# Moving the second matrix's threshold of one group from the mixing stage into the inverse rounds

## The chip, the cores and the metric

One core of a Trainium2 chip runs the program. Its five engines work through instruction queues of their own: PE (matrix products), DVE, ACT and POOL (elementwise work) and SP, which here only issues DMAs. An instruction starts when it is at the head of its engine's queue and everything it waits for is done. The metric is the device time of one execution in microseconds.

## What is computed

Four layers act in turn on a tensor of 4 images x 64 channels x 256 x 256 in float32. Layers 0, 2 and 3 are long convolutions along rows and columns with generated filters, plus a bias times the input; the kernel computes them as products with Toeplitz matrices. Layer 1 is the one that the change touches:

```python
f1 = haar2d(x)
acc = jnp.zeros_like(f1[:, :conv_w.shape[1]])
for i in range(v.shape[0]):
    f3 = f1 * v[i]
    f4 = jnp.einsum('bchw,oc->bohw', f3, conv_w[i])
    f5 = jnp.sign(f4) * jax.nn.relu(jnp.abs(f4) - tau[i])
    acc = acc + f5
y = haar2d(acc, inverse=True)
return y + x
```

`v[i]` and `tau[i]` depend on the position in the image only, not on the channel, so the product with `v[i]` may come after the channel mixing as well as before it. `sign` times `relu(abs - tau)` is the shrinking (soft threshold) that the title speaks of. There are two matrices, and the last addition of x is done in the Haar domain too.

## The kernel before

The four images are two groups of two. A **round** holds two channels of the two images of a group, 128 partitions x 8 blocks x 256 columns; there are 32 rounds per group, 64 in all. Three pieces of program are woven together:

- `phase_a` (lines 405 to 505): for each round the first convolution and the forward Haar transform. It writes Haar coefficients to a tensor `coef` in device memory, one per group.
- `phase_b` (507 to 678): the channel mixing. It needs all channels of a position, so it goes through `coef` in 64 **steps** per group, each of 128 partitions x 2 images x 512 positions. A step is two **units**, one for each of the two matrices. A unit is a product with the matrix on PE (`mix`), then on a tile of 128x1024: the product with v (`multiply`, DVE), `sign` and `magnitude` (ACT), the subtraction of tau (`less`, DVE), the threshold (`threshold`, DVE, a scalar_tensor_tensor), and the addition (`add`, POOL; for the first unit the addition of x in two halves, for the second one addition of 128x1024). `store` writes the step's sum to a tensor `mixed`. Each unit is three entries in a list; `exchange` is a copy on ACT, once a step. `load_f` and `load_v` bring the next steps' coefficients, v and tau, two DMAs for the coefficients and one each for v and tau.
- `phase_c` (680 to 808): for each round the inverse Haar transform and the two last convolutions. It loads g from `mixed`, undoes the free-axis part of the Haar transform on POOL (`inverse_free`, line 340: sixteen additions and subtractions, a pair per level, each level twice as long as the one before, the last two of 128x1024), with scalings of g's parts on ACT (line 353) ahead of each level, does the partition part on PE (`product`, c0ps), and then per layer a row stage (`rows`, c1r and c2r) and a column stage (`columns`, c1c and c2c) on PE. Row results are copied out of PSUM by ACT (line 733), column results by DVE with the bias term (line 752), Haar results by ACT and, for the second group, half by DVE (line 721).

The order of every engine's queue is the order in which this program writes its instructions. A round of `phase_c` is eighteen pieces: four of c1r, one Haar product, four of c2r (of the round before), the other Haar product, four of c1c, four of c2c. At the start of a piece `flush` writes the PSUM copies that the piece before left waiting; then come loads and stores, the PE work, and one step of the inverse Haar of the round two further on (`step(t + 2, 1)`, two pieces per level). `sums(t + 2)`, in the round's first piece, sets that inverse Haar up.

PSUM banks for the convolutions come in pairs from `rings`: during the mixing of the second group two pairs, in the last stage four (`rings[:] = [acps, acps, wide, wide]`). A product waits until the pair it is to write has been copied out.

`beside` weaves two lists: it spreads the second list's entries evenly over the first's. The mixing of the first group runs beside the forward rounds of the second. The mixing of the second group runs beside the first `cut_c` pieces of the inverse rounds:

```python
cut_a, cut_c = (ROUNDS + 2) * A_PIECES + BLOCKS + 1, (ROUNDS - 2) * C_PIECES
...
beside(main, phase_b(1), len(c_first) + len(a_end) + 2 * BLOCKS, 0)
during.close()
wide = pool("wide2", 4, space=PSUM)
rings[:] = [acps, acps, wide, wide]
beside(c[cut_c:], [], 0, 0)
```

So 30 of the inverse rounds run beside mixing; the others, with what is left of the last, run alone. That is the last stage.

## Time and profile before

| what | value |
|---|---|
| median of 3 runs | 2615.12 us (2614.1 to 2617.48) |
| the profiled execution | 2622.7 us, of which the span from the first to the last instruction 2620.6 us |
| busy share of the span: PE, DVE, ACT, POOL | 90%, 64%, 51%, 74% |
| granted PE clock, mean | 0.965 |
| moved by DMA | 631.58 MB, 241 GB/s in the mean |
| issues of v and tau | 128 each, 512 KB each, 5.9 and 6.6 us to landing |
| issues of mixed (stores), g (loads) | 256 each, 256 KB each, 5.9 and 5.5 us to landing |

The span has four stretches: forward rounds of the first group (to some 450 us), forward rounds of the second beside mixing of the first (to some 1130 us), inverse rounds beside mixing of the second group (to some 1950 us), and inverse rounds alone (to the end). In lines of the profile, L579 stands for line 579 of the kernel; `out<-in` names tiles; `x` ahead of a number is a count.

### The profile page before, as it was taken

Reading aid. Unit: us, or ns where it says so; the run is one execution under the profiler, and the core shown is the slowest. Engines: PE = TensorE matmul, PEld = TensorE weight load, DVE = VectorE, ACT = ScalarE, POOL = GpSimd, SP = SyncE. Lnnn points to the kernel's source line nnn. Section 1 sums busy time; section 2 is a strip of 40 time slices with the busy share of each in tenths; the row PEclk is TensorE's granted clock in tenths of the full one; section 3 lists DMA queues with packets and bytes.
Section 4 is the critical chain, followed back from the end, with each engine's and each line's share of the span. In section 5 each row is a group of like instructions: output and inputs, shape, how many; then the busy total and the mean of one; then the engine's idle time right before and its main releaser. Section 6 shows DMA issues by size and latency. Waiting matters only on the chain.

```text
span 2620.6 us, 120068 instructions
## 1 busy us (share of the span) xinstructions
PE 2357.1 (90%) x53276; PEld 1908.0 (73%) x53276; DVE 1686.6 (64%) x1972; ACT 1325.3 (51%) x2169; POOL 1951.1 (74%) x2422
## 2 busy tenths in 40 slices
PE   6989999678878778768999999999999999999999
PEld 4777777445544445546877777787789999999999
DVE  2464445799999999736877878878763333333333
ACT  1111112566666656426777776778763443434432
POOL 2877887888989989858888878888876565565661
PEclk9999999899899888979999999999999999999999
DMA  5756887698999889556888878888865544445442
GB/s 147 252 193 221 254 261 275 232 332 326 336 332 335 319 316 331 186 190 216 286 310 288 295 273 288 274 285 286 284 231 181 171 143 153 159 141 166 148 137 86
DMA packets 241180, 631.58 MB, mean 241 GB/s; under 512 B 42758, under 2 KB 125351, under 8 KB 224536
## 3 DMA queue, kind: packets, MB, share of 16 engines
q1 hardware_dynamic: 240664, 623.92, 69.4%
q8 instruction: 419, 6.86, 1.1%
q14 instruction: 97, 0.79, 0.1%
HBM read 412.59 MB, written 211.16 MB: 238 GB/s over the span
## 4 chain that ended last, share of the span: by engine, by line
PE 42%; DVE 12%; DMA 10%; POOL 9%; ACT 6%; issue 5%; SPq 2%; DVEq 0%; ACTq 0%; POOLq 0%
PE c1c L285 9%; PE c2r L285 9%; PE c2c L285 8%; PE c1r L285 8%; PE c0ps L297 3%; DVE a L605 3%; PE f L579 3%; DVE x L594 3%; POOL f L335 2%; POOL fw L333 2%; DVE m L608 2%; DMA ft<-coef 2%; ACT a L602 2%; DMA mixed<-gt 2%; DVE x L449 2%
## 5 line engine op out<-in xcount | busy, mean ns | idle before, releaser
L370 POOL TENSOR_TENSOR i<-i,g 128x16 f32<-128x16 f32 x744 | 395.1, 550 | 378.9 <-ACT g L353 359.9
L579 PE MATMUL f<-ft,mix 64*64 64x512 f32 x2048 | 326.4, 642 | 106.7 <-DVE x L594 84.5
L285 PEld LDWEIGHTS a1ps<-tx,x 64*64 64x64 f32 x8192 | 303.4, 140 | 132.9 <-DVE f L462 47.8
L602 ACT ACTIVATE a<-x 128x1024 f32<-128x1024 f32 x256 | 264.5, 1033 | 205.6 <-DVE m L608 205.6
L285 PE MATMUL a1ps<-tx,x 64*64 64x192 f32 (+3 forms) x8192 | 341.5, 309 | 29.3 <-DVE f L462 15.3
L605 DVE TENSOR_TENSOR a<-a,tau 128x1024 f32<-128x1024 f32 x256 | 314.3, 1228 | 79.9 <-ACT a L602 77.5
L285 PEld LDWEIGHTS c2r<-tx,cy 64*64 64x64 f32 x8192 | 319.1, 135 | 62.2 <-ACT ch L733 28.8
L598 ACT ACTIVATE m<-x 128x1024 f32<-128x1024 f32 x256 | 271.9, 1062 | 173.3 <-DVE x L594 112.4
L594 DVE TENSOR_TENSOR x<-f,v 128x1024 f32<-128x1024 f32 x256 | 311.7, 1218 | 61.1 <-PE f L579 56.4
L285 PEld LDWEIGHTS c1c<-ty,ch 64*64 64x64 f32 x8192 | 311.3, 133 | 53.4 <-ACT ch L733 29.8
L285 PE MATMUL c2r<-tx,cy 64*64 64x64 f32 (+3 forms) x8192 | 330.9, 301 | 13.6 <-ACT ch L733 10.9
L285 PE MATMUL c1r<-tx,z 64*64 64x128 f32 (+3 forms) x8192 | 326.7, 299 | 13.1 <-DMA tx<-filt 6.7
L285 PEld LDWEIGHTS c1r<-tx,z 64*64 64x64 f32 x8192 | 303.0, 134 | 46.4 <-issue 26.4
L285 PEld LDWEIGHTS a2ps<-ty,ay 64*64 64x64 f32 x8192 | 281.4, 135 | 74.1 <-issue 27.2
L285 PE MATMUL a2ps<-ty,ay 64*64 64x256 f32 (+3 forms) x8192 | 319.1, 301 | 12.5 <-ACT ay L429 9.1
L285 PE MATMUL c1c<-ty,ch 64*64 64x192 f32 (+3 forms) x8192 | 321.1, 298 | 7.0 <-ACT ch L733 6.2
L608 DVE SCALAR_TENSOR_TENSOR m<-a,m 128x1024 f32<-128x1024 f32 x256 | 313.0, 1223 | 19.5
L429 ACT COPY ay<-a1ps 128x512 f32<-128x512 f32 x256 | 137.0, 587 | 370.7 <-PE a1ps L285 370.3
L285 PE MATMUL c2c<-ty,ch 64*64 64x192 f32 (+3 forms) x8192 | 316.4, 297 | 3.6 <-issue 3.6
L285 PEld LDWEIGHTS c2c<-ty,ch 64*64 64x64 f32 x8192 | 303.2, 133 | 22.4 <-issue 10.9
L449 DVE SCALAR_TENSOR_TENSOR x<-x,bias_sb,a2ps 128x512 f32<-128x512 f32 x256 | 179.4, 743 | 214.1 <-POOL f L335 132.1
L620 POOL TENSOR_TENSOR gt<-gt,m 128x1024 f32<-128x1024 f32 x128 | 303.2, 2369 | 11.7 <-DVE m L608 10.2
(69 smaller groups left out, 3193.9 us busy)
## 6 DMA issues: line engine op xcount, KB each, us to landing
coef<-f SPq DMA_DIRECT2D x256, 256.0 KB, 4.4
ft<-coef SPq DMA_DIRECT2D x256, 256.0 KB, 6.2
v<-in_v SPq DMA_DIRECT2D x128, 512.0 KB, 5.9
tau<-in_tau SPq DMA_DIRECT2D x128, 512.0 KB, 6.6
mixed<-gt SPq DMA_DIRECT2D x256, 256.0 KB, 5.9
g<-mixed SPq DMA_DIRECT2D x256, 256.0 KB, 5.5
x<-in_x SPq DMA_DIRECT2D x63, 1024.0 KB, 8.5
out<-o SPq DMA_DIRECT2D x63, 1024.0 KB, 5.1
```

Source lines behind the costliest of these rows:

```text
L285: nc.tensor.matmul(ps[r][half(c), j % 2, k * ROW :], data[half(r), c, k, bass.ts(j, ROW)], t(r, c)[:, : N - k * ROW], start=k == 0, stop=k ...
L297: nc.tensor.matmul(ps[r][half(c)].rearrange("p h k -> p (h k)"), matrix[half(r)], pairs(r, c).rearrange("p h k -> p (h k)"), start=True, s ...
L370: engine.tensor_tensor(to, s, d, op)
L429: later(lambda y=y, ps=ps: nc.scalar.copy(y, ps))
L449: nc.vector.scalar_tensor_tensor(to, old, bias_sb[:, c : c + 1], ps, ALU.mult, ALU.add)
L579: nc.tensor.matmul(un[u]["f4"][half(q), b, :], mixers[0][half(r), bass.ts(i, C)], st[s]["f"][half(r), b], start=True, stop=True, tile_posi ...
L594: nc.vector.tensor_tensor(un[u]["x"], un[u]["f4"], both(u, "v"), ALU.mult)
L598: nc.scalar.activation(un[u]["m"], un[u]["x"], AF.Sign)
L602: nc.scalar.activation(un[u]["a"], un[u]["x"], AF.Abs)
L605: nc.vector.tensor_tensor(un[u]["a"], un[u]["a"], both(u, "tau"), ALU.subtract)
L608: nc.vector.scalar_tensor_tensor(un[u]["m"], un[u]["a"], 0.0, un[u]["m"], ALU.max, ALU.mult)
L620: nc.gpsimd.tensor_tensor(st[s]["g"], st[s]["g"], m, ALU.add)
```

## The change

For the second group, and for steps from `FULL` = 2 on, the second unit of a step no longer shrinks. Its product with the matrix is copied from PSUM to a tile `raw` by DVE and stored to a new tensor `unshrunk`; v, sign, magnitude, tau, threshold and addition are left out there. For the second matrix v and tau are no longer loaded in those steps. For the first two steps the second unit is done as before, and zeros are stored in `unshrunk`. (These two steps are joined with one another in `join` and `part`.)

In the last stage the rounds of the second group load their rows of `unshrunk` (`load_raw`), and `shrink` does the product with v, sign, magnitude, subtraction and threshold in two halves of 128x1024, in the pieces of the round three ahead (`AHEAD`), with tiles of v and tau in the rounds' own layout that are loaded once (`v_rows`, `tau_rows`). `x`, the intermediate, lies in PSUM, one buffer of two banks. `sums` adds the two halves to g on POOL before the inverse Haar.

Mixing of the second group now runs beside 29 inverse rounds, not 30. The last stage has three pairs of PSUM banks, not four. The load of g for round 32 is no longer set apart.

```diff
-    cut_a, cut_c = (ROUNDS + 2) * A_PIECES + BLOCKS + 1, (ROUNDS - 2) * C_PIECES
+    cut_a, cut_c = (ROUNDS + 2) * A_PIECES + BLOCKS + 1, (ROUNDS - AHEAD) * C_PIECES
...
+        def raw(u):
+            return grp == GROUPS - 1 and u % 2 == 1 and FULL <= u // 2 < STEPS
...
+                d[name] = []
+                for i in range(2 if s < FULL else 1):
+                    t = bp.tile([P, W], F32, tag=f"{name}{i}", name=f"{name}{i}_{grp}_{s}", bufs=3 - 2 * i)
+                    d[name].append(t)
+                    nc.sync.dma_start(t, bass.AP(src.tensor, at + i * W, [[n, P], [1, W]]))
...
         def multiply(u):
+            if raw(u):
+                t = st[u // 2]["raw"] = bp.tile([P, NB, W], F32, tag="raw", name=f"raw_{grp}_{u}", bufs=2)
+                nc.vector.tensor_copy(t, un[u]["f4"])
+                return
...
         def store(s):
             for to, g in step_of(mixed[grp], s, st[s]["g"]):
                 nc.sync.dma_start(to, g)
+            if grp == GROUPS - 1:
+                if s < FULL:
+                    t = st[s]["raw"] = bp.tile([P, NB, W], F32, tag="raw", name=f"none_{grp}_{s}", bufs=2)
+                    nc.gpsimd.memset(t, 0.0)
+                for to, g in step_of(unshrunk, s, st[s]["raw"]):
+                    nc.sync.dma_start(to, g)
...
+        def load_raw(t):
+            if alone <= t < total:
+                r = st[t]["raw"] = late["sb"].tile([P, 2 * M, N], F32, tag="raw", name=f"raw_{t}", bufs=2)
+                for rows, to in all_rows(unshrunk, t % ROUNDS, r):
+                    nc.sync.dma_start(to, rows)
+
+        def shrink(t, j):
+
+            if j < 0 or not alone <= t < total:
+                return
+            h, j = divmod(j, SHRINK)
+            s = st[t]
+            at = [s[k].rearrange("p (s b h) k -> p s b (h k)", s=2, b=NB)[:, h] for k in ("raw", "shrunk") if k in s]
+            if j == 0:
+                if h == 0:
+                    s["shrunk"] = late["sb"].tile([P, 2 * M, N], F32, tag="shrunk", name=f"shrunk_{t}", bufs=2)
+                s["x"] = late["ps"].tile([P, NB, W], F32, tag="x", name=f"x_{t}_{h}")
+                nc.vector.tensor_tensor(s["x"], at[0], late["v"][:, h].unsqueeze(1).to_broadcast([P, NB, W]), ALU.mult)
+            elif j == 1:
+                nc.scalar.activation(at[1], s["x"], AF.Sign)
+            elif j == 2:
+                nc.scalar.activation(s["x"], s["x"], AF.Abs)
+            elif j == 4:
+                by = late["tau"][:, h].unsqueeze(1).to_broadcast([P, NB, W])
+                nc.vector.tensor_tensor(s["x"], s["x"], by, ALU.subtract)
+            elif j == 5:
+                nc.vector.scalar_tensor_tensor(at[1], s["x"], 0.0, at[1], ALU.max, ALU.mult)
...
         def sums(t):
             if t < total:
                 s = st[t]
+                if t >= alone:
+                    for h in range(2):
+                        to, of = (s[k].rearrange("p (s n) k -> p s (n k)", s=2)[:, h] for k in ("g", "shrunk"))
+                        nc.gpsimd.tensor_tensor(to, to, of, ALU.add)
                 s["ci"] = big("t1", f"ci_{t}", 2)
...
-                if t == alone - 2:
-                    load(alone)
                 sums(t + 2)
...
-            if j == 2 * BLOCKS and t + 3 != alone:
+            if t >= alone - AHEAD:
+                if j == 0 and t == alone - AHEAD:
+                    load_raw(alone)
+                if j == BLOCKS:
+                    load_raw(t + AHEAD + 1)
+                shrink(t + AHEAD, order.index(j) - 2)
+            if j == 2 * BLOCKS:
...
-    wide = pool("wide2", 4, space=PSUM)
-    rings[:] = [acps, acps, wide, wide]
+    rings[:] = [acps, acps, pool("wide2", 2, space=PSUM)]
+    late["sb"] = pool("late", 1)
+    late["ps"] = pool("late_ps", 1, space=PSUM)
+    for name, src in (("v", v_rows), ("tau", tau_rows)):
+        t = late[name] = late["sb"].tile([P, 2, W], F32, tag=name, name=f"{name}_rows")
+        for r in range(2):
+            nc.sync.dma_start(t[half(r)].rearrange("p s w -> p (s w)"), src)
     beside(c[cut_c:], [], 0, 0)
```

`AHEAD` is 3, `SHRINK` 8, `FULL` 2. In the later steps the guards `if raw(u): return` stand in `sign`, `magnitude`, `less`, `threshold` and `add` as well.

## The prediction

> **What bounds the kernel now.** I first read the page's forty slices to find the stages, then busy time by stretch. The first line below is the stretch in which the second group's mixing runs beside the first group's inverse rounds; the second is the last stage, inverse rounds alone. Columns: stretch, its length, then busy us and instruction count (x) of PE, PEld, DVE, ACT, POOL, then granted clock, DMA share, GB/s.
>
> ```profile
> 1200.00:1950.00 750.00, 706.77 (x15688) 579.78 (x15684) 592.12 (x599) 563.34 (x908) 628.78 (x643) 0.99 0.80 279
> 1957.00:2572.00 615.00, 612.96 (x16807) 587.97 (x16803) 222.87 (x318) 246.75 (x547) 364.25 (x512) 1.00 0.49 153
> ```
>
> An inverse round issues 528 matmul records (four times 128 in the convolutions, 16 in the Haar product). The last stage holds 16807/528 = 31.8 rounds, **19.3 us each**, with PE idle for 2 us of 615: PE sets the end there. In the mixing stretch the side list has 404 pieces for 532 main pieces, which is 13.67 per round or 2.28 steps (a step is six pieces, two units); with 16 records a step a round has 564, so 15688/564 = 27.8 rounds, **27.0 us each**. PE, DVE, POOL and ACT are all 75 to 94% busy there: no single engine, but queues in fixed order that wait on each other.
>
> Next the order of time in one round of the last stage, since an engine's queue order decides what new work costs there.
>
> ```profile
> 2214.11 4.02 POOL L370 TENSOR_TENSOR i<-i,g 128x256 f32<-128x256 f32 x4 [1.37 <-ACT g L353]
> 2214.32 1.71 ACT L353 ACTIVATE g<-g 128x512 f32<-128x512 f32 x3
> ...
> 2218.20 4.72 POOL L370 TENSOR_TENSOR ci<-i,g 128x1024 f32<-128x1024 f32 x2
> ...
> 2221.97 4.48 PE L285 MATMUL c1r<-tx,z 64*64 64x256 f32 x124
> 2222.17 1.41 DVE L752 SCALAR_TENSOR_TENSOR o<-cy,bias_sb,c2c 128x512 f32<-128x512 f32 x2 [0.78 <-PE c2c L285]
> ...
> 2224.41 1.07 ACT L733 COPY ch<-c1r 128x512 f32<-128x512 f32 x2 [8.38 <-PE c1r L285]
> ...
> 2227.10 4.58 PE L285 MATMUL c2r<-tx,cy 64*64 64x256 f32 x125
> ```
>
> PE starts a round at 2221.97 and its second row stage 5.1 us later. POOL finishes the previous inverse Haar at 2222.92, 0.95 us *into* the round. ACT's third scaling in the row at 2214.32 is already the first of the next round's: ACT runs ahead, then idles 8.38 us. Two more views, groups by shape and SP's rows in order of time:
>
> ```profile
> L620 POOL TENSOR_TENSOR gt<-gt,m 128x1024 f32<-128x1024 f32 x128 | 303.2, 2369 | 11.7 <-DVE m L608 10.2 <-POOL gt L624 0.3
> L594 DVE TENSOR_TENSOR x<-f,v 128x1024 f32<-128x1024 f32 x256 | 311.7, 1218 | 61.1 <-PE f L579 56.4 <-DMA tx<-filt 4.6
> L598 ACT ACTIVATE m<-x 128x1024 f32<-128x1024 f32 x256 | 271.9, 1062 | 173.3 <-DVE x L594 112.4 <-POOL gt L620 28.7 <-POOL gt L624 12.5
> L602 ACT ACTIVATE a<-x 128x1024 f32<-128x1024 f32 x256 | 264.5, 1033 | 205.6 <-DVE m L608 205.6
> ```
>
> ```profile
> 1499.33 1.70 SPq L692 DMA_DIRECT2D g<-mixed  x2
> 1501.23 3.11 SPq L149 DMA_DIRECT2D tx<-filt  x4
> 1504.46 1.59 SPq L149 DMA_DIRECT2D ty<-filt  x2
> 1506.10 2.50 SPq L149 DMA_DIRECT2D tx<-filt  x4
> 1508.70 2.06 SPq L149 DMA_DIRECT2D ty<-filt  x2
> 1510.85 1.18 SPq L629 DMA_DIRECT2D mixed<-gt  x2
> ```
>
> SP issues 16 DMAs in 12.7 us, back to back, 0.79 each.
>
> **What leaves the mixing stretch.** Of a step's second unit go three DVE instructions (product 1.22, subtraction 1.23, threshold 1.22), sign and magnitude on ACT (1.06 + 1.03) and one POOL addition (2.37). In their place comes one DVE copy from PSUM, which this trace does not show at 128x1024: between the product of that shape, 1.22, and twice the 128x512 copy, 1.38; I take 1.22, the nearer in shape. Net per step: DVE 2.45, ACT 2.1, POOL 2.4. The two zero tiles for steps 0 and 1 are one memset each on POOL, about 1.15 us by elements from the 80x320 memset of 0.36 us, hidden in POOL's 16% of idle; without that cover 2 us.
>
> What it adds there: SP. A step issues six DMAs now (ft, mixed two each, v and tau one each) and eight after, two stores more; v and tau are halved, so the bytes stay. And the stretch is one round shorter (29 rounds beside mixing, not 30): 404/514 x 18/6 = 2.36 steps per round. With 17 DMAs of the inverse round itself (12 filters, 4 g, 1 out) SP issues 17 + 2.36 x 8 = **35.9 per round**, against 17 + 2.28 x 6 = 30.7 now. At the back-to-back price above that is 28.4 us; at the best row (4 in 2.50 us, with the gap to the next 0.65 each) 23.3. PE's floor is the 19.3 plus 4.72 units at 0.76 to 1.09 us (a Haar product's stretch alone; the eight mixing records end to end): 22.9 to 24.4. Now SP's 30.7 fit in 27.0, so not all are 0.79. I take 0.71 for a DMA, midway, and **25.5 us per round**, SP the last to finish; bounds 23.3 and 27.0 (no gain). Behind SP's queue stand ft, v, tau, g and the filters, which all wait when it is full.
>
> Stretch: 28 rounds x 27.0 = 756 become 27 x 25.5 = 688.5, and one round, the first alone, at about 24: 19.3 plus 5 (bounds 0 and 12), because the first product in it waits for the last store to land (5.9 us in the table of DMA issues), then for a load (5.5), with the DVE evacuations queued behind it. Together **-43.5**; with both bounds -108 and +4.
>
> **What the last stage receives.** In each of 32 rounds: on DVE two products, subtractions and thresholds (7.3 us), on ACT two signs and magnitudes (4.2), on POOL two additions, 4.72 us as the row at 2218.20; on SP four loads, 21 DMAs x 0.8 = 17 us of a round, issued a round ahead. By busy sums all fits: POOL 364/31.8 = 11.5 + 4.7 = 16.2, ACT 7.8 + 4.2, DVE 7.0 + 7.3. PSUM rings go from four bank pairs to three.
>
> By order it does not fit. The two additions stand at the head of a round on POOL, behind the previous Haar's tail; the first ACT scaling of that round (L353, on the same g) must wait for both; behind it on ACT stand the evacuations of c1r, which free the banks of the second row stage, and the later scalings, which POOL's tail waits for. So there is a **loop**, POOL to ACT to POOL, and its length is a floor for the round:
>
> - additions: 4.7;
> - ACT from the first scaling to the sixth: 6 scalings (0.23 to 0.65, 2.2 in all), 8 evacuations of 0.59, 2 z copies of 0.60, 2 signs of 1.06, 1 magnitude of 1.03 = 11.3, less 19 overlaps of 0.11 (copies at 2224.41 are 1.07 for two): 9.2. The second sign waits for the second product, which on DVE follows subtraction, threshold and a z copy, all after the magnitude: +0.6;
> - POOL's last four operations: 2 x 1.28 + 4.72 = 7.2.
>
> Sum **21.8**, against 19.3. ACT cannot run ahead any more; PE waits some 2.5 us at its second row stage.
>
> One thing more. The moved product reads raw and v, both from SBUF; before, every large DVE operation beside POOL had one operand in PSUM. The trace has DVE operations with two SBUF operands, with POOL still (first row) and with POOL busy:
>
> ```profile
> 129.17 2.14 DVE L205 SCALAR_TENSOR_TENSOR u<-k,u 128x512 f32<-128x512 f32 x3
> 158.61 2.07 POOL L335 TENSOR_TENSOR f<-x 128x1024 f32<-128x1024 f32 x1
> 158.97 5.16 DVE L205 SCALAR_TENSOR_TENSOR u<-k,u 128x512 f32<-128x512 f32 x3
> ```
>
> Three take 2.14 us in the one case and 5.16 in the other: they take turns with POOL. In the new round the first product falls among POOL's tail or additions, which run without a gap, so POOL loses its 1.2 us; the second falls where POOL has gaps. Loop **23.0** (bounds 21.2, with neither wait, and 23.6, with both products paid).
>
> The Trainium skill, page "SBUF — State Buffer", section "SBUF: two separate sides", calls this an exclusive lock: a DVE operation with two SBUF inputs and a GpSimd one that reads SBUF exclude each other for a whole instruction. By that rule both products would cost POOL 1.2 us whenever POOL is busy, 24.2 a round, some 38 us more than my sum. The page "DMA: Bandwidth & Descriptors", section "Issuing engines are not separate DMA queues", holds the time to initiate a DMA to be usually small; by it SP would drop out and the mixing round stand at PE's 23 to 24 us, 50 us below my sum; the SP rows above speak against it.
>
> Last stage: 32 x (23.0 - 19.3) = **+118** (bounds +61 and +138).
>
> **Sum.** -43.5 + 118 = +75. The profiled execution ran 2622.7 us with a span of 2620.6, and the runs' median is 2615.1, so on the median: 2615 + 75 = **2690 us**.
>
> **Rivals.**
> *A, the other side: the loop does not close.* If POOL's additions fit into its idle (41% of the last stage, 7.9 us a round, more than 4.7) and the last stage keeps 19.3, the mixing stretch at 24 us a round decides: 27 x 24 + 24 - 756 = -84, **2531**. For it: busy sums, and DVE, ACT and POOL all get lighter beside mixing. Against: POOL's idle lies after ACT's scalings ("<-ACT g L353"), not before them. It decides once 32 x (loop - 19.3) is below 732 - 27r for a mixing round r: at r = 25.5 a loop below 20.7, at 23.3 below 22.5.
> *B, SP fills up.* Mixing stays at 27.0 a round: -3 + 118, **2730**. For: 0.79 each, 28.4 us. Against: a lighter POOL and DVE end the waits inside SP's queue sooner.
> *C, no turns with POOL.* DVE's product finds a gap: loop 21.8, +80 - 43.5, **2652**. For: ACT waits long enough for a late product; against: the rows above.
>
> **Chances.** Forecast (2670 to 2715) 0.42, B 0.20, C 0.20, A 0.15, and 0.03 for gain and loss to cancel. The range reaches from the near edge of cancelling to past B: 2612 to 2745, which leaves out A and a little above. A measurement of this kernel tells about 0.2% (5 us) from no change: faster 0.15, same 0.03, slower 0.82.
>
> **What would show it.** In the changed profile the last stage's c1r stages should stand 22 to 23.5 us apart; the second row stage should wait for ACT; ACT's first scaling should wait for a POOL addition; POOL should be over 70% busy with its tail running straight into the additions; the products should last over 1.22 us wherever POOL runs. In the mixing stretch SP should issue almost without gaps and a round take 24.5 to 26.5. I am wrong if c1r stays 19 to 20 us apart, or if the mixing round falls below 24.

## The result, and the profile after

| | before | after |
|---|---|---|
| median of 4 runs each | 2616.3 us (2614.1 to 2618.02) | **2900.16 us** (2899.37 to 2903.64) |
| ratio after/before, 95% interval | | **1.109** (1.107 to 1.111): slower by 284 us |
| span of the profiled execution | 2620.6 us | 2897.6 us |
| granted PE clock, mean | 0.965 | 0.926 |
| start to round 2 | 1200.9 us | 1206.6 us |
| rounds 2 to 28, beside mixing, mean | 27.02 us | **29.73 us** |
| round 29 | 26.9 us | 27.0 us |
| rounds 30 to 61, mean | 19.21 us | **25.40 us** |
| round 62 to the end | 48.7 us | 48.7 us |

A round is measured from ACT's first copy of c1r in one round to that in the next. Of the 277 us by which the span grew, 198 lie in rounds 30 to 61 (32 x 6.19), 73 in rounds 2 to 29, 6 before. The forecast had the two parts at +118 and -43.5: slower was right, but the last stage grew by 80 us more than forecast, and the stretch that was to get faster got slower, which is 117 us more.

The two stages by busy time, in the columns of the prediction (stretch, length, busy us and count of PE, PEld, DVE, ACT, POOL, then clock, DMA share, GB/s):

```profile
1206.00:2009.00 803.00, 699.74 (x15266) 555.15 (x15262) 442.77 (x466) 433.97 (x763) 476.16 (x565) 0.94 0.78 264
2036.00:2849.00 813.00, 694.23 (x16834) 620.38 (x16838) 470.02 (x503) 361.26 (x671) 568.30 (x575) 0.90 0.48 153
```

Beside mixing, DVE fell from 79% busy (592 of 750) to 55%, ACT from 75% to 54%, POOL from 84% to 59%. The work did leave, and the stretch still took longer. In the last stage PE was busy all the time before and is idle 119 us of 813 now, and its clock is 0.90 where it was 1.00.

**The last stage.** Waits of after, 2036 to 2849 us (engine, line, what it waited for: us in all, times, longest):

```profile
ACT g L357 <- POOL g L767: 357.3, 32, 11.2
...
DVE x L753 <- ACT x L750: 203.9, 31, 8.7
...
PE c2r L289 <- ACT ch L800: 121.4, 32, 3.9
...
ACT ch L800 <- PE c2r L289: 51.5, 55, 2.4
ACT shrunk L748 <- DVE x L746: 44.4, 30, 1.5
```

Once a round ACT's first scaling (L357) waits some 11 us for POOL's additions (L767), and PE's second row stage 3.8 us for ACT's evacuations. That is the loop. The same in order of time, one turn, from the last copies of c2r in the turn before:

```profile
2400.51 1.08 ACT L800 COPY ch<-c2r 128x512 f32<-128x512 f32 x2 [0.89 <-PE c2r L289]
...
2402.98 1.07 ACT L800 COPY ch<-c2r 128x512 f32<-128x512 f32 x2 [1.18 <-PE c2r L289]
...
2404.51 2.40 POOL L374 TENSOR_TENSOR i<-i,g 128x256 f32<-128x256 f32 x2 [1.70 <-ACT g L357]
2404.53 1.80 DVE L746 TENSOR_TENSOR x<-raw,v_rows 128x1024 f32<-128x1024 f32 x1
...
2406.36 1.03 ACT L748 ACTIVATE shrunk<-x 128x1024 f32<-128x1024 f32 x1 [1.52 <-DVE x L746]
2407.28 0.62 ACT L357 ACTIVATE g<-g 128x512 f32<-128x512 f32 x1
...
2408.05 2.52 POOL L374 TENSOR_TENSOR i<-i,g 128x512 f32<-128x512 f32 x2 [1.14 <-ACT g L357]
...
2410.64 4.71 POOL L374 TENSOR_TENSOR ci<-i,g 128x1024 f32<-128x1024 f32 x2
...
2414.56 1.89 DVE L746 TENSOR_TENSOR x<-raw,v_rows 128x1024 f32<-128x1024 f32 x1
...
2415.31 5.62 POOL L767 TENSOR_TENSOR g<-g,shrunk 128x1024 f32<-128x1024 f32 x2
...
2420.97 0.23 ACT L357 ACTIVATE g<-g 128x16 f32<-128x16 f32 x1 [11.18 <-POOL g L767]
...
2421.10 1.05 ACT L800 COPY ch<-c1r 128x512 f32<-128x512 f32 x2
...
2421.72 4.59 PE L289 MATMUL c2r<-tx,cy 64*64 64x256 f32 x74 [3.89 <-ACT ch L800]
```

POOL's tail (2408.05 to 2415.35) runs straight into the additions (to 2420.93), and within 0.2 us ACT's scaling and evacuations start, and PE soon after. Over 29 such turns the three legs measure 7.27 us (tail), 5.60 (additions; the first 3.30, the second 2.33) and 12.75 (from the end of the additions to the next tail). The forecast had 7.2, 5.9 and 9.8.

In that last row 74 matmuls take 4.59 us, where the prediction's row had 125 in 4.58. Slices of 5 us of after, behind the pause before the turn shown (it ends at 2395.57) and behind the one in it (to 2421.72); the first number behind the counts is the granted clock:

```profile
2395.00:2400.00 5.00, 4.43 (x62) 3.91 (x66) 1.02 (x1) 4.62 (x10) 1.39 (x7) 0.50 0.56 169
2400.00:2405.00 5.00, 5.00 (x122) 4.43 (x120) 2.52 (x4) 3.15 (x7) 1.73 (x5) 0.91 0.18 42
2405.00:2410.00 5.00, 5.00 (x152) 4.80 (x148) 4.43 (x6) 3.42 (x4) 3.86 (x4) 1.00 0.06 14
...
2420.00:2425.00 5.00, 3.28 (x44) 2.80 (x48) 0.00 (x0) 4.03 (x9) 2.22 (x7) 0.66 0.68 219
2425.00:2430.00 5.00, 5.00 (x137) 4.58 (x132) 3.49 (x4) 3.92 (x10) 1.92 (x5) 1.00 0.22 56
```

After each such pause PE is granted half its clock, by the trace's clock rows in turn for some 5.4 and 3.1 us: 62 records in 4.4 us of work where full speed does some 150 in 5.

**Beside mixing.** Waits of after, 1206 to 2009 us:

```profile
...
ACT m L618 <- DVE x L612: 189.9, 25, 12.8
...
DVE raw L609 <- DMA unshrunk<-raw: 133.1, 24, 12.4
POOL gt L652 <- DVE m L634: 88.9, 30, 6.1
...
PE f L593 <- DVE raw L609: 49.0, 20, 5.5
```

The second line shown is new, and the others grew beside it (before, from 1200 to 1950 us, ACT waited 53.1 us for x and POOL 8.8 for m): the copy to raw has two buffers, and it waits for the store of the raw tile of two steps earlier. While it stands at the head of DVE's queue, everything behind it waits. One such wait on DVE, and what SP issued meanwhile:

```profile
1545.01 1.22 DVE L609 COPY raw<-f 128x1024 f32<-128x1024 f32 x1
...
1549.80 1.23 DVE L612 TENSOR_TENSOR x<-f,v 128x1024 f32<-128x1024 f32 x1 [1.10 <-PE f L593]
1558.25 1.23 DVE L609 COPY raw<-f 128x1024 f32<-128x1024 f32 x1 [7.22 <-DMA unshrunk<-raw]
```

```profile
1541.45 3.41 SPq L727 DMA_DIRECT2D g<-mixed  x4
1544.90 2.52 SPq L153 DMA_DIRECT2D tx<-filt  x4
1547.46 1.23 SPq L153 DMA_DIRECT2D ty<-filt  x2
1548.74 2.84 SPq L153 DMA_DIRECT2D tx<-filt  x4
1551.68 1.17 SPq L153 DMA_DIRECT2D ty<-filt  x2
1552.95 1.93 SPq L658 DMA_DIRECT2D mixed<-gt  x2
1554.92 1.25 SPq L664 DMA_DIRECT2D unshrunk<-raw  x2
```

The raw tile was copied from 1535.20 on, but its store was issued at 1554.92: it is written behind the store of mixed, and here sixteen DMAs of the inverse round came first, back to back.

### The profile page after: what moved, and what is told of

Its sections match the earlier page's. It is cut to its first block, busy times and chain, and to the rows that moved or that the text cites. A ratio compares the mean times of both kernels' runs of the same rounds, so it can differ in the third digit from the quotient of the medians.

```text
span 2897.6 us, 120326 instructions
## 1 busy us (share of the span) xinstructions
PE 2451.0 (85%) x53276; PEld 1941.7 (67%) x53276; DVE 1800.6 (62%) x2040; ACT 1323.6 (46%) x2173; POOL 2018.7 (70%) x2426
## 4 chain that ended last, share of the span: by engine, by line
PE 28%; POOL 23%; DVE 12%; DMA 11%; issue 10%; ACT 9%; SPq 7%; DVEq 0%; POOLq 0%; ACTq 0%
PE c2r L289 10%; POOL g L767 6%; POOL f L339 4%; POOL fw L337 4%; POOL ci L374 3%; PE c2c L289 3%; PE a1ps L289 3%; PE a2ps L289 3%; PE c1r L289 3%; SPq L153 3%; PE f L593 2%; DVE a L629 2%; DVE x L453 2%; ACT g L357 2%; PE c1c L289 2%
## 5 line engine op out<-in xcount | busy, mean ns | idle before, releaser
L289 PE MATMUL c2r<-tx,cy 64*64 64x256 f32 (+3 forms) x8192 | 392.7, 339 | 128.1 <-ACT ch L800 127.0
L289 PEld LDWEIGHTS c2r<-tx,cy 64*64 64x64 f32 x8192 | 355.0, 155 | 212.7 <-ACT ch L800 180.2
L357 ACT ACTIVATE g<-g 128x16 f32<-128x16 f32 x434 | 198.5, 463 | 372.4 <-POOL g L767 357.3
L289 PE MATMUL a1ps<-tx,x 64*64 64x64 f32 (+3 forms) x8192 | 346.3, 312 | 25.0 <-DVE f L466 14.1
L618 ACT ACTIVATE m<-x 128x1024 f32<-128x1024 f32 x194 | 205.8, 1061 | 307.3 <-DVE x L612 249.3
L289 PE MATMUL c1c<-ty,ch 64*64 64x128 f32 (+3 forms) x8192 | 326.0, 300 | 6.4 <-ACT ch L800 5.8
L289 PEld LDWEIGHTS c1r<-tx,z 64*64 64x64 f32 x8192 | 295.5, 137 | 52.3 <-issue 29.2
L374 POOL TENSOR_TENSOR ci<-i,g 128x1024 f32<-128x1024 f32 x124 | 291.8, 2374 | 10.2 <-issue 3.2
L629 DVE TENSOR_TENSOR a<-a,tau 128x1024 f32<-128x1024 f32 x194 | 238.1, 1228 | 50.4 <-ACT a L624 49.6
L612 DVE TENSOR_TENSOR x<-f,v 128x1024 f32<-128x1024 f32 x194 | 236.1, 1217 | 43.4 <-PE f L593 42.1
L819 DVE SCALAR_TENSOR_TENSOR cy<-z,bias_sb,c1c 128x512 f32<-128x512 f32 x256 | 179.3, 742 | 129.0 <-PE c1c L289 129.0
```

The source lines that it names most:

```text
L289: nc.tensor.matmul(ps[r][half(c), j % 2, k * ROW :], data[half(r), c, k, bass.ts(j, ROW)], t(r, c)[:, : N - k * ROW], start=k == 0, stop=k ...
L357: nc.scalar.mul(diffs(half), diffs(half), math.sqrt(half))
L374: engine.tensor_tensor(to, s, d, op)
L612: nc.vector.tensor_tensor(un[u]["x"], un[u]["f4"], both(u, "v"), ALU.mult)
L618: nc.scalar.activation(un[u]["m"], un[u]["x"], AF.Sign)
L629: nc.vector.tensor_tensor(un[u]["a"], un[u]["a"], both(u, "tau"), ALU.subtract)
```

## The experiments

Times in us; "mixing" and "last" are the mean rounds 2 to 28 and 30 to 61. A single run beside the kernel before on the same chip (2609 to 2621), except where an interval stands. Edits are to the changed kernel unless they say "before". What the edits leave alone shows the noise of a single run: the mixing round is 29.73, 29.66, 29.62 and 29.86 in after, e3_no_add, e5_late_start and e6_one_operand, whose mixing code is the same, and 27.02 and 26.86 in before and e4_ring3, so differences of some 0.2 us tell nothing.

| kernel | what | time | mixing | last |
|---|---|---|---|---|
| before | | 2616.3 | 27.02 | 19.21 |
| after | | 2900.2 | 29.73 | 25.40 |
| e3_no_add | POOL's additions left out | 2700.29 | 29.66 | 19.48 |
| e5_late_start | inverse Haar begins later in the round | 2698.46 | 29.62 | 19.50 |
| e6_one_operand | moved product with one SBUF operand | 2845.97 | 29.86 | 23.62 |
| e4_ring3 | before, three bank pairs in the last stage | 2615.63 | 26.86 | 19.31 |
| e1_raw4 | four raw buffers | 2856.52 | 27.81 | 25.3 |
| e2_store_act | raw stores issued by ACT | 3007.96 | 33.71 | 25.35 |
| e12_sooner | raw stores one step sooner | 2866.51 | 28.13 | 25.3 |
| e7_one_dma | one DMA for two in a step's loads and stores | 2883.41 | 29.19 | 25.35 |
| e10_all | e1, e5 and e7 together | 2636.26 | 26.69 | 19.61 |
| e14_all | and e12 | 2637.13 | 26.78 | 19.49 |
| e9_before_one_dma | before, e7's edit | 2623.11 | 27.14 | 19.25 |
| e15_small_v | e10, a sixteenth of v and tau's bytes | 2616.43 | 26.19 | 19.61 |
| e16_before_small_v | before, a sixteenth of v and tau's bytes | 2606.41 | 26.62 | 19.15 |
| e17_half_mix | e10, half of the mixing products | 2637.85 | 26.61 | 19.51 |
| e18_before_half_mix | before, half of the mixing products | 2616.15 | 26.86 | 19.23 |
| e19_half_filters | e10, half of the filter loads | 2624.88 | 26.45 | 19.51 |
| e20_before_half_filters | before, half of the filter loads | 2613.85 | 26.75 | 19.11 |
| e21_all_less | e15, e17 and e19 together | 2585.08 | 25.24 | 19.51 |

### The loop in the last stage

**e3_no_add** takes POOL's additions out of the loop, **e5_late_start** keeps them and moves the start of the inverse Haar, and with it ACT's first scaling, from the second piece of the round to the sixth, with two steps a piece for a while:

```diff
-                        nc.gpsimd.tensor_tensor(to, to, of, ALU.add)
+                        pass
```

```diff
-            if j > 0:
-                step(t + 2, 1)
+            k = order.index(j)
+            if t + 2 < alone:
+                step(t + 2, 1 if k else 0)
+            elif k >= 5:
+                step(t + 2, 2 if k < 10 else 1)
```

> The two POOL additions of the shrunk halves to g at the head of each round of the last stage are left out; everything else of the shrinking is done. Theory (a loop of POOL's additions, ACT's scalings and POOL's tail): the last stage's round falls from 25.4 to 19.3-20 us, the granted clock there from 0.90 back to 1.0, time 2900 - 32 x 5.7 = about 2720. Rival (three pairs of banks, or DVE's shrinking ahead of the evacuations): the round stays above 22 us, time above 2790. The mixing stretch is unchanged by both.

> The additions stay; in the last stage the inverse Haar's steps start at the sixth piece of a round, two steps a piece until the tenth, so the first ACT scaling is queued behind the evacuations of c1r and the first half's sign and magnitude. Theory: PE no longer waits at its second row stage for long, the loop is shorter by what ACT does before that scaling (some 3.8 us) and by the slowed clock; round 19.5-21.5 us, time 2710 to 2775. Rival (POOL's own work, 11.5 + 4.7 and the turns with DVE, is the floor whatever the order): round above 23, time above 2825.

Busy time in the last stage of e3_no_add, then of e5_late_start:

```profile
2034.00:2650.00 616.00, 611.80 (x16726) 566.60 (x16719) 444.56 (x501) 357.11 (x657) 424.19 (x504) 1.00 0.63 202
```

```profile
2034.00:2650.00 616.00, 611.67 (x16720) 576.02 (x16716) 473.83 (x500) 352.81 (x654) 565.69 (x564) 1.00 0.63 203
```

Both bring the round back to 19.5 us, with PE busy throughout and its clock at 1.00. e5_late_start is the one that decides: it leaves no work out, POOL is 92% busy (565.69 of 616), and the round is PE's again. It is the order, not POOL's work, that cost nearly all of the 198 us (the round is 19.50 for 19.21 before): with the evacuations of c1r no longer queued behind the scaling that waits for the additions, nothing closes the loop.

**e6_one_operand** replaces the moved product by one with a constant, so that it reads a single SBUF tile:

```diff
-                nc.vector.tensor_tensor(s["x"], at[0], late["v"][:, h].unsqueeze(1).to_broadcast([P, NB, W]), ALU.mult)
+                nc.vector.tensor_scalar(s["x"], at[0], 0.5, None, ALU.mult)
```

> In the changed kernel the last stage's product of raw with v is a product with a constant, so it reads one tile of SBUF, not two; v of the second group's second matrix is left out of the result there. Theory (DVE and POOL take turns when DVE reads two SBUF operands): the product lasts 1.2 us everywhere (1.8-1.9 before), the first addition 2.33 us (3.32 before), the loop loses 1.0 for the addition and 0.6 before the second sign, round 23.3-24.2, time 2855 to 2835. Rival (the longer rows are waits that cost nothing): round within 0.4 of 25.4, time above 2885.

Groups of the last stage of after, and below them of e6_one_operand (busy us, mean ns of one):

```profile
L767 POOL TENSOR_TENSOR g<-g,shrunk 128x1024 f32<-128x1024 f32 x63 | 176.0, 2813 | 0.0
...
L746 DVE TENSOR_TENSOR x<-raw,v_rows 128x1024 f32<-128x1024 f32 x61 | 110.9, 1819 | 0.0
...
L374 POOL TENSOR_TENSOR i<-i,g 128x256 f32<-128x256 f32 x64 | 75.2, 1196 | 49.7 <-ACT g L357 49.7
```

```profile
L767 POOL TENSOR_TENSOR g<-g,shrunk 128x1024 f32<-128x1024 f32 x57 | 133.2, 2361 | 0.0
...
L746 DVE TENSOR_SCALAR x<-raw 128x1024 f32<-128x1024 f32 x56 | 68.2, 1219 | 0.0
...
L374 POOL TENSOR_TENSOR i<-i,g 128x256 f32<-128x256 f32 x56 | 39.8, 732 | 36.0 <-ACT g L357 36.0
```

With two SBUF operands the product takes 1.82 us where it takes 1.22. On POOL it is the addition (2.81 for 2.36) that meets the first product, and the operation of 128x256 (1.20 for 0.73) that meets the second. The round falls by 1.8: 0.9 on POOL's leg (additions 4.67 for 5.60), 0.85 on ACT's (11.9 for 12.75), where the second sign waits some 0.5 less for the product and the copies of c2r some 0.3 less for PE. The turns are real and are paid twice; they are not the main cost.

**e4_ring3** gives the kernel before three bank pairs in its last stage:

```diff
-    wide = pool("wide2", 4, space=PSUM)
-    rings[:] = [acps, acps, wide, wide]
+    wide = pool("wide2", 2, space=PSUM)
+    rings[:] = [acps, acps, wide]
```

> The kernel before with three pairs of PSUM banks in the last stage, not four, and nothing else of the change. Theory (the loop over POOL and ACT costs the last stage, not the banks alone): the last stage's round stays at 19.2-19.3 us, time within 5 us of before. Rival (the lost bank pair makes PE wait on the evacuations): round above 19.8, time over 20 us longer.

19.31 against 19.21: the lost bank pair costs 0.1 us a round at most while the evacuations come in time.

### The wait for the raw store

**e1_raw4** gives raw four buffers (and, for the room, x one and m two in the second group). **e2_store_act** issues the raw stores from ACT, **e12_sooner** issues them at the next step's beginning, ahead of the copy, and **e7_one_dma** makes one DMA of the two for ft, for mixed and for raw, so that SP has five in a step for eight. The edits in this order:

```diff
-                t = st[u // 2]["raw"] = bp.tile([P, NB, W], F32, tag="raw", name=f"raw_{grp}_{u}", bufs=2)
+                t = st[u // 2]["raw"] = bp.tile([P, NB, W], F32, tag="raw", name=f"raw_{grp}_{u}", bufs=4)
...
```

```diff
                 for to, g in step_of(unshrunk, s, st[s]["raw"]):
-                    nc.sync.dma_start(to, g)
+                    nc.scalar.dma_start(to, g)
```

```diff
             if j == 0:
+                if i == 0 and grp == GROUPS - 1 and FULL <= s - 1 < STEPS:
+                    store_raw(s - 1)
                 if u < units:
                     multiply(u)
...
```

```diff
-            by_e = images.rearrange("(m e) b w -> e m (b w)", e=CI)
-            at = [ap.offset + (e * STEPS // 2 + s // 2) * PAIR + s % 2 * P // CI * n for e in range(CI)]
-            return [(bass.AP(ap.tensor, at[e], [[n, P // CI], [1, n]]), by_e[e]) for e in range(CI)]
+            at = ap.offset + s // 2 * PAIR + s % 2 * P // CI * n
+            rows = bass.AP(ap.tensor, at, [[n, P // CI], [STEPS // 2 * PAIR, CI], [1, n]])
+            return [(rows, images.rearrange("p b w -> p (b w)"))]
```

> The raw tiles of the mixing stretch have four buffers, not two (x one and m two for the second group, to make room). Theory: the copy to raw stands at the head of DVE's queue waiting for a store of two steps before to land, and this sets the mixing round. Then that wait (114 us in the stretch from 1300 to 1980) goes, the round falls from 29.7 to 25.5-26.5 us, and the time from 2900 to about 2800 (27 rounds x 3.7). Rival: SP issues too much, 35.9 DMAs a round, whatever the buffers: the wait moves to ft or the filters, the round stays above 28.5 and the time above 2865. The last stage stays at 25.4 us a round by both.

> The two stores of raw per step are issued on ACT's queue, not on SP's; two raw buffers as in the changed kernel. SP is left with 2.36 x 6 + 17 = 31.2 DMAs a round. Theory (a store late on SP, a buffer short): the stores no longer stand behind twelve filter loads, land in time, and the mixing round falls to 25.5-26.5; time about 2800. Rival (two buffers are short however the store is issued, since it takes 5 us to land): the wait of DVE for the store stays above 60 us and the round above 28.

> The changed kernel with the two stores of raw issued one step sooner (after the step's own copy, not with the stores of mixed two steps on); same 35.9 DMAs a round, two raw buffers. Theory (a ring: DVE's copy waits for a store, the store stands on SP behind ft's load, that waits for POOL's addition, that for DVE's threshold behind the copy): the wait of DVE for the store falls from 114 us to under 40 and the round from 29.7 to the price of a full SP, 27.3-28.2, time 2840 to 2860. Rival (the store itself takes too long for two buffers): wait above 80 us, round above 29.

> In the changed kernel each of a step's transfers of 512 KB (ft, mixed, unshrunk) is one DMA, not two of 256 KB, in both groups' mixing; two raw buffers. SP is left with 17 + 2.36 x 5 = 28.8 DMAs a round, the bytes are the same. Theory (SP's queue is full and sets the mixing round): the round falls from 29.7 to 25-27 us, DVE's wait for the raw store from 114 us to under 40, time 2775 to 2830. Rival (the bytes or the landing time, not the number of issues): round above 28.5, time above 2865.

In e1_raw4 the wait is gone and the round falls by 1.9 us, to a place between the two that were expected, but a new one stands in its place, here in its waits from 1210 to 1980 us:

```profile
DVE x L612 <- DMA v<-in_v: 85.2, 23, 7.7
```

SP is now the one that is late: worked out from its rows from 1250 to 1850 us, the gaps of over 0.2 us between its issues come to 20 of 600 us. e12_sooner likewise falls to 28.1 with SP idle for some 15 us, though the wait for the store is still 111 us there (it was expected below 40), so a wait's microseconds are not the price of the wait. e7_one_dma cuts SP's DMAs of a round from 35.9 to 29 and leaves it idle for some 125 us, and gains only 0.5 us, with 121 us of wait for the store: fewer issues help little while the store still comes two steps later.

e2_store_act went the other way, by 4.0 us a round, which neither side expected. ACT of e2_store_act in order of time:

```profile
1493.57 0.27 ACT L357 ACTIVATE g<-g 128x64 f32<-128x64 f32 x1
1499.36 2.02 ACTq L664 DMA_DIRECT2D unshrunk<-raw  x2
1501.47 1.07 ACT L800 COPY ch<-c2r 128x512 f32<-128x512 f32 x2 [7.62 <-DMA mixed<-gt]
```

ACT does nothing from 1493.84 to 1499.36, stands at the store for two more, and only then evacuates c2r, on which PE waits 4.3 us. What the store stood waiting for, the semaphore events of the trace tell. (A semaphore is a counter that a DMA raises when it lands, and for which instructions wait.) The program's DMAs take eight semaphores in turn, some 365 DMAs each, whichever engine issues them. 104 of the 106 store DMAs on ACT from 1210 to 1980 us wait for the very semaphore that they raise themselves, that is, until the DMA that took it before has landed. For the store at 1499.36 that was a filter load that SP had issued at 1496.26, which landed at 1499.34. Ahead of 70 of these stores ACT's idle time was ended so, by the landing of a DMA of SP's; it sums to 147 us, some 6 us a round. A store on an engine that evacuates PSUM made PE wait here for DMAs that have nothing to do with it.

So the new wait costs about 1.9 to 2.5 us a round (29.7 to 27.8 with SP full; 29.2 in e7_one_dma to 26.7 in e10_all below, with SP less loaded), and SP's queue the rest.

### All mends together

**e10_all** is e1_raw4, e5_late_start and e7_one_dma in one kernel; **e14_all** has e12_sooner's edit as well.

> Four raw buffers, one DMA for each of ft, mixed and unshrunk, and the late start of the inverse Haar in the last stage. Theory (the mixing round is held by two things in turn, the short buffers and the full SP, and each alone frees little): the round falls to 25-26.3 us, the last stage stays at 19.5, time 2696 - 27 x 3.9 = about 2590 (2570 to 2610), less than before. Rival (something else, such as PE's clock after its pauses or the bytes): round above 27.3, time above 2630.

> As the run with four buffers, one DMA each and the late start, and the raw stores issued a step sooner. Theory: with four buffers the store is no longer late, so the earlier issue is worth little: within 10 us of that run. Rival (the ring through SP still closes): 15 us or more below it.

e10_all: 2636.26 us, ratio to before 1.008 (1.005 to 1.010); e14_all the same within 1 us, ratio 1.008 (1.005 to 1.011). 264 us of the loss are back, but the expected 2590 was missed by 46: some 26 us of it in the mixing rounds (26.7, where the sum had 25.7), 11 in round 29 (32.8 us for 21.4 in e5_late_start), 3 in the last stage. Against before, e10_all gains 9 us in the mixing rounds and loses 13 in the last stage (0.3 to 0.4 us a round), 6 in round 29 and 4 ahead of round 2. Round 29 goes from 21 us (e3_no_add) to 41 (e1_raw4) over the runs, and why was not looked into. Waits of e10_all, 1210 to 1980 us:

```profile
...
ACT m L618 <- DVE x L612: 118.4, 32, 8.3
ACT ch L800 <- PE c1r L289: 111.6, 38, 8.3
DVE cy L819 <- PE c1c L289: 97.6, 39, 7.8
...
DVE x L612 <- DMA v<-in_v: 46.0, 14, 5.8
```

The store is off the list; ACT waits for DVE, and both wait for PE. No version was found that beats the kernel before.

### What sets the mixing round

A third to a half of what DVE, ACT and POOL do for mixing is gone in e10_all and the round is 0.3 us shorter, little more than the noise. Three causes were taken down one by one, in e10_all and in the kernel before. Fewer issues in the kernel before (**e9_before_one_dma**, the diff of e7_one_dma), fewer bytes (**e15_small_v**, **e16_before_small_v**), less mixing work on PE (**e17_half_mix**, **e18_before_half_mix**), and a fifth fewer DMAs (**e19_half_filters**, **e20_before_half_filters**); **e21_all_less** has the last three kinds at once. The edits, in this order, as made to the changed kernel:

```diff
-                    nc.sync.dma_start(t, bass.AP(src.tensor, at + i * W, [[n, P], [1, W]]))
+                    nc.sync.dma_start(t[:, :32], bass.AP(src.tensor, at + i * W, [[n, P], [1, 32]]))
...
```

```diff
         def mix(u):
+            if raw(u):
+                return
...
-                nc.vector.tensor_copy(t, un[u]["f4"])
+                nc.vector.tensor_copy(t, un[u - 1]["f4"])
```

```diff
         def filters(t, l):
-            if t < total:
+            if 2 < t < alone and t % 2:
+                st[t]["toep", l] = st[t - 1]["toep", l]
+            elif t < total:
                 st[t]["toep", l] = load_toeplitz(l, t)
```

> The kernel before with ft and mixed as one DMA of 512 KB each, 17 + 2.28 x 4 = 26.1 issues a round, not 30.7. Theory (SP, busy 86%, does not yet set the round before): mixing round 26.3-27.0, time 2595 to 2620. Rival (SP sets it before too): round below 25.5, time below 2575.

> The run with four buffers, one DMA each and the late start, and in the second group's mixing v and tau are loaded for 32 columns only, which stand for all: as many issues as there, 0.46 MB less a step (of 2.1), so 1.1 MB less a round (of some 7.8). The other columns of v and tau are left out of the second group's first matrix. Theory (the mixing round is held by what the DMA engines move, share 0.83, and SP's issues are long because of it): round from 26.7 to 23.5-24.8 us, time 2636 - 27 x 2.5 = 2550 to 2585. Rival (the number of issues): round above 26.3, time above 2625.

> The kernel before, with v and tau of the second group loaded for 32 columns of each matrix only, which stand for all: same issues, DVE, ACT and POOL work as before, 0.98 MB less a step. The other columns of v and tau are left out there. Theory A (the mixing stretch before was held by the DMA engines, not by DVE, ACT and POOL): round from 27.0 to 24.5 or less, time below 2550. Theory B (as in the prediction: the queues of DVE, ACT and POOL in their fixed order hold it): round above 26.3, time above 2595.

> e10_all, and for the second group the mixing product with the second matrix is left out in the steps that store raw rows (the copy to raw reads the product with the first matrix again), which leaves out 2.36 mixing units a round on PE and nothing on any other engine or queue. PE busy per unit is about 1.27 us (151 us for 119 units in the kernel before). Theory PE: PE's own work (25 us of a 26.7 us round) sets the mixing round, so it falls by 2.4 to 3.0 us to 23.7 to 24.3 us, and the run to about 2636 - 27 x 2.7 = 2563 us (2555 to 2572). Theory queues: SP's 31 DMAs and the waits in the written order set it, PE only follows; the round stays at 26 us or above, and the run above 2617 us.

> The kernel before, and for the second group the mixing product with the second matrix is left out (the multiplication with v reads the product with the first matrix again), which leaves out 2.28 mixing units a round on PE and nothing elsewhere. Theory PE: the mixing round falls from 27.0 to 24.1 to 24.6 us, the run by 67 to 80 us to about 2545 us. Theory queues and elementwise engines: the round stays within 0.7 us of 27.0 and the run above 2600 us, and what the change took off DVE, ACT and POOL could have been worth something.

> e10_all, and in the stretch beside mixing every second inverse round takes the filters of the round before instead of loading its own, which leaves out 6 of the 28.6 DMAs that SP issues in a round and nothing on another engine. Theory SP: its queue (532 of 600 us used in e10_all) sets the 26.7 us round, which falls to PE's own 25.0 to 25.7, the run to about 2600 us. Theory interlock: no engine or queue alone sets it; the waits among queues of fixed order do; the round stays at 26.2 us or above and the run above 2620 us.

> The kernel before with the same edit (6 of 30.7 DMAs of a round left out). Theory SP: 27.0 falls to 26.0 or below, the run below 2590 us. Theory interlock: 26.5 to 27.1, the run within 15 us of 2616.

> e10_all with three things left out at once: half of the filter loads (as e19_half_filters), the second mixing product in the steps that store raw rows (as e17_half_mix), and 7/8 of the bytes of v and tau (as e15_small_v). If PE, SP and bytes each stand close behind one another, so that taking one alone shows nothing, the round now falls to 22.5 to 24.0 us and the run below 2560 us. If it stays above 25.5 us, what sets it is none of the three and lies in the written order and its waits.

(32 of 512 columns of v and tau are loaded in the steps in question, so it is 15/16 of the bytes that this leaves out, not 7/8.)

Merged DMAs give the kernel before nothing (27.14). Bytes give 0.4 to 0.5 us. Halving PE's mixing work gives 0.1 to 0.2, which is within the noise, where 2.4 to 3.0 were expected had PE's work set the round. Half of the filter loads give 0.2 to 0.3, hardly more; SP is then idle for some 170 of 600 us in e19_half_filters. The wait for the landing of the DMA that had an issue's semaphore before is not the bound either: it is some 60 of 600 us on SP in e10_all and 6 in e19_half_filters. All together give 1.45 us, which is neither the 22.5 to 24.0 of several bounds close behind one another nor above 25.5. The same 600 us, of e10_all, of e17_half_mix and of e21_all_less:

```profile
1250.00:1850.00 600.00, 562.47 (x12744) 461.05 (x12740) 372.09 (x393) 365.43 (x638) 389.13 (x464) 0.99 0.84 293
```

```profile
1250.00:1850.00 600.00, 543.15 (x12482) 453.22 (x12478) 373.84 (x397) 366.95 (x643) 393.41 (x474) 0.97 0.84 296
```

```profile
1250.00:1850.00 600.00, 562.13 (x13124) 471.93 (x13118) 394.52 (x418) 388.52 (x683) 412.46 (x498) 0.99 0.74 255
```

PE looks 91 to 94% busy in all three, whether it has 16 or 8 mixing records a step, while the others are 61 to 69% busy. A busy share is not a floor: with half of the mixing records gone (their own busy time fell from 130.0 to 74.1 us) only 19 us of PE's 562 went, since the other records took up more time, at a clock of 0.97 for 0.99. What is shown is that no engine's work, no queue's issues and no bytes, as far as they were taken down, set this round alone. That it is the waits among queues of fixed order is what remains, and it was not shown directly; no kernel with another weave was run.

## Why the prediction was right and wrong

Three steps failed: the length of ACT's part in the loop (12.75 us for 9.8), the copy to raw, whose wait was not in the sum (1.9 to 2.5 us a round), and the gain that work taken off beside mixing was to bring (at most 0.3 us a round for 1.5).

- **The loop** was right in mechanism and in three of its signs: the second row stage waits for ACT, ACT's first scaling for POOL's additions, POOL's tail runs into them, and POOL is 70% busy in the stage. e3_no_add and e5_late_start show it from two sides. The size was off: 23.0 forecast, 25.4 measured. The mis-sized term is the second, "ACT from the first scaling to the sixth", 9.2 + 0.6 = 9.8, which measured **12.75**. In it ACT waits 1.4 us a round for the second product (44.4 / 32; the 0.6 of the forecast) and 1.6 us for PE's c2r (51.5 / 32), which was not in the sum at all: 2.4 of the 2.95 us. The rest is ACT's own work, some 9.6 for 9.2. The wait for c2r was put at nothing without a reason; the last stage of before has it too (72.4 us in 62 waits), but there ACT has time to spare. That the half clock makes it, the turns themselves show, for the loop's turns alternate: where PE runs 5.4 us at 0.50 after its pause, ACT waits 2.1 us for c2r and the turn, from one start of c2r to the next, takes 26.2; where it runs 3.1 us so, ACT waits 0.9 and the turn takes 25.1 (medians of 16 turns each). A turn of e6_one_operand whose pause of 2.4 us was followed by no half clock, at 2109.1 us, has a wait of 0.16 us; the turns behind it there, with 3.4 us of half clock after as long a pause, have 1.35. The other two terms held: 7.27 for 7.2, 5.60 for 5.9.
- **The turns** of DVE and POOL were right: 1.82 us for 1.22 and 3.30 for 2.36 on the first addition. Their price is 1.8 us a round (e6_one_operand), not the 1.2 of the sum: POOL's leg lost 0.9, and the second product, held up too, delays ACT's second sign. The forecast let the second product find a gap, but POOL's pair of 128x256 at 2404.51 takes 2.40 us beside it, so both products meet POOL, as the Trainium skill's rule has it ("SBUF — State Buffer", section "SBUF: two separate sides"); POOL loses 0.9 us at each (3.30 for 2.36, 2.40 for twice 0.73), not the 1.2 drawn from the rule, but the 24.2 us a round by it was nearer than 23.0. The bound of 23.6 "with both products paid" left out the 0.6 us of its own second term; with it the sum is 24.2 as well.
- **The mixing stretch**, 25.5 us a round, was wrong in sign. The step that failed is "In their place comes one DVE copy from PSUM": it was costed as 1.22 us of DVE, and its wait was not asked for. The copy needs a free raw buffer, that needs the store two steps back, and that stands on SP behind a round's loads: 133 us of wait, 1.9 to 2.5 us a round (e1_raw4, e10_all). The bounds of 23.3 and 27.0 had no room for a new wait, and so the range ended too low.
- **SP's price** was wrong too, but decided less than thought. 728 DMAs from 1250 to 1850 us kept SP occupied for some 550 us, 0.755 each and 27.1 a round for 35.9, against 0.71 and 25.5; that is rival B's round. Yet with SP's load cut to 29 the round fell only to 29.2 (e7_one_dma), so SP alone was not the end of it. The Trainium skill ("DMA: Bandwidth & Descriptors", "Issuing engines are not separate DMA queues") calls the time to initiate a DMA "usually small relative to the DMA itself", and so it is here, 0.75 us against 4.8 to landing (the raw stores of after); the prediction read it as small beside a round, which the page does not say and 35.9 such issues are not. The 23 to 24 us of that reading no run reached, not even e19_half_filters with SP a quarter idle.
- **That removed work buys time** beside mixing was the deeper error. Even mended (e10_all), taking 2.45 us of DVE, 2.1 of ACT and 2.4 of POOL a step out is worth 0.3 us a round at most, not 1.5. "Queues in fixed order that wait on each other" stood in the prediction's reading of before; its sum did not follow from it.
- **Round 29**, the first alone, took 27.0 us for the 24 forecast. The 6 us before round 2 were not looked into; the kernel before in e4_ring3 and e9_before_one_dma began round 2 between 1194 and 1197 us, so such a difference also lies between its own runs.
- **Rivals.** A (2531) fell: the loop closes, and the mixing round did not fall to 24. B (2730) had SP's price right (27.1 us a round for its 27.0) and missed the wait. C (2652) fell with e6_one_operand. None had a wait for the new store.

## What to carry to other kernels

Where a change adds a copy into a buffer that a DMA empties, ask first when that store is issued and what stands ahead of it on its queue; two buffers were too few for a store that comes two steps later behind sixteen loads, and everything behind the copy on its engine paid. Before a DMA is moved to another engine's queue, look which earlier DMA its issue has to wait for. When work is added to a round, follow the order of each queue through a whole turn: POOL had the time for the additions, but at the head of the round they tied three engines into a loop, and beginning the dependent work four pieces later took 200 us off. Where many engines are 75 to 95% busy in a fixed order, do not count on what taking work off some of them should save until a run shows what ends the round; here it saved 0.3 us of the 1.5 forecast.

## What the runs showed of the hardware

- **The PE clock in a loop.** The pauses of 3.9 us in the last stage were followed in turn by some 5.4 and 3.1 us at 0.50 (stretches of 6.83 and 3.41 us, which begin shortly before the pause ends), so the stage's clock was 0.90; without the pauses (e3_no_add, e5_late_start) it was 1.00. The Trainium skill, "TensorE: Matmul & The Clock Gate", "Part 1: The HAM clock gate", states that PE needs some 3.4 us of sustained work to get from half to full rate; stretches of once and twice 3.41 us agree with that. Here the slow matmuls lay in the loop, and so the pause was paid again by ACT's wait for them.
- **A DMA issued from ACT** held ACT's work up for 7.62 us at one store (e2_store_act), 5.5 of it before the issue is recorded, and the edit cost 4 us a round. The store waited for the landing of a DMA of SP's that had used its semaphore before it, as 104 of 106 did: the eight semaphores tie the two engines' queues together.
- **The price of an issue on SP is not set by bytes.** An issue of v took 0.74 us in the kernel before, 0.96 in e10_all with half the bytes (256 KB for 512), and 1.07 in e15_small_v with 16 KB; and at the same 256 KB it took 0.73 in after (all from 1250 to 1850 us).
